# A decoder of state-space scan, cross attention and experts on one core: keys and values made a batch ahead, w2 as seven half-size products, C product in tiles of its own

## The chip, the core and the metric

The kernel runs on one core of a Trainium2 chip. The metric is the device time of one execution in microseconds. The engines of the core run side by side, each with its own instruction queue: TensorE (PE, with its weight loads PEld), VectorE (DVE), ScalarE (ACT), GpSimd (POOL), and SyncE (SP), which here does nothing but issue DMAs. They wait for each other through semaphores. A median is over three runs; the profile is one further execution with every instruction recorded.

## What is computed

Everything is fp32. The input x has 8 batches of 512 tokens of 512 features. Three layers follow one another, each with a sum and a layer norm:

```python
x = layernorm(x + mamba(x))                     # res_scale * (y @ out_proj) + x inside, so 2x + ...
x = layernorm(x + xattn(x, ctx, ctx, mask))
x = layernorm(x + ffn(x))

# mamba: 1024 channels d, 16 states n, token by token
h   = exp(A * dt_t) * h + dt_t * B_t * x_t      # h[d, n]
y_t = sum_n h[d, n] * C_t[n]
# xattn: 16 heads of 32; keys and values come from ctx alone
q, k, v = x @ Wq.T + bq, ctx @ Wk.T + bk, ctx @ Wv.T + bv
# ffn: 32 experts, 4 for each token, at most 640 tokens for an expert
h   = silu(xe @ w1) * (xe @ w3)
out = (h @ w2) * weight                         # added to the token's row
z   = silu(x @ sw1) * (x @ sw3) @ sw2           # the shared expert, for every token
```

## The kernel before

The program has three stages.

**layers** does the scan layer, and beside it attention, the shared expert and the choice of experts. The scan layer runs over 16 chunks, two of 256 tokens for each batch (t = 0 and t = 1). A chunk has 32 steps: for each of 8 groups of 128 channels (c) and each of 4 groups of four states (g). On the 128 partitions lie 64 channels, twice, with two states in each half; so a step's tile h is 128 x (4 x 257), the first column of each row being the state that is carried in. One step is, by engine and line:

- ACT copies the carried state into h's first columns (`carry`, L440; from `state` at t = 1, from zeros at t = 0) and makes the four decays of the next step with Exp (`decays`, L434), into one of two tiles.
- DVE multiplies dt·x with the broadcast B into h (L446), runs the recurrence over h in place (`scan`, L450), at t = 0 copies h's last columns to `state` (L452), and multiplies h by the broadcast C in place (`collect`, L467).
- PE sums the states with eight products of 256 columns into the PSUM tile py (L471).

h has four buffers. The broadcasts of B and C (`bc`, four buffers) come from a scratch in DRAM by SP's DMAs, two steps ahead; the copies of dt and dt·x over the partition halves (`both`) go the same way. Between the steps the loop puts the work around the scan at fixed steps: the gate product (L483), the output projection of the chunk before (L500), the input projections of this chunk's gate and of the next chunk (L302), the convolution (L336), dt (`prepare`).

Attention and the shared expert of batch b − 1 are a list of small pieces, `units(b - 1)`, each with a weight near its PE time. While batch b is scanned, the loop takes pieces from the list as fast as the weights say, so that the list ends with the batch's second chunk. Batch 0 has no such list, and `units(7)` runs after the last chunk, with nothing beside it. A list does, in this order: load Wv and the context (transposed, cT); four products for the values, copied by ACT into `l_va` (L690: per key and pair of heads 32 values, 32 ones, 32 values); four for the keys, to the tile kT with bias and mask (products L682, DVE L702); the first rows of x1, the scan layer's result, from DRAM (`fetch`); their transposes (L676, copy L677); four for the queries; then by pairs of heads `spread` (L722 to L725), which copies queries and keys by DMA into tiles with extra rows for the mask and the maximum, scores and maxima (L735, L737), scores transposed and exponentials (L761, L765), the product with the values (L777); output projection; the shared expert; the choice of experts (`choose`, `locate`); and `send`, which scatters each row to its experts' slots in the buffer xbuf. Large tiles of the list share four slots, s1 to s4: cT and the attention's result are in s2, x1T and then x2's rows in s1, the queries and then the shared expert's hT in s3, kT and then x2T in s4. Every 512 x 512 weight goes through one tile name, wa, with two buffers, loaded one weight ahead.

**experts** goes through the 32 experts. The 640 rows of an expert are loaded at once (xe, L1104) with w1, w3 and w2 (1 MB each, L1107), one expert ahead. `hidden` makes silu(x·w1)·(x·w3) with seven block products instead of eight (Strassen's scheme in Winograd's form) for both weights: 320 columns in each product (L1152), the sums of weight blocks on DVE (`sums_w`, L1127) and of x blocks (`sums_x`, L1144 to L1147), partial sums kept by ACT (L1166) and joined by DVE (L1173, L1177). `give` does the product with w2 in the plain way, five tiles of 128 rows by four products of 512 columns (L1218); ACT scales each tile by the routing weights (L1222) and POOL adds it by an indirect DMA to the tokens' rows in `based` (L1223). Before each of these five tiles PE transposes one tile of the next expert (`flip`, L1136; DVE's copy L1137), and DVE makes one of w3's sums. Each of the five scatters waits for the one before, and an expert's xe tile is read by its scatters until the end, for the row numbers lie in it.

**finish** loads the 4096 rows, and normalizes and stores them (L1266, L1269).

The order of the instructions on each engine is the order in which the program issues them, with a product's use put off by one piece of work (`do`, `settle`); a few places first finish all that is put off (`dry`). The lines of the functions that the change touches follow.

## Time and profile before

| | us |
|---|---|
| median of three runs | 5657.23 (5656.19 to 5658.22) |
| the profiled execution | 5660.41 |
| its span | 5658.7 |

The span is what the profiler saw from the first to the last instruction; mean granted clock of PE 0.937 of full speed.

| stage | from us | to us |
|---|---|---|
| constants, first projections | 0 | 84.9 |
| batch 0, two chunks, nothing beside the scan | 84.9 | 436.4 |
| batch 1 | 436.4 | 901.9 |
| batches 2 to 7, each with attention of the batch before | 901.9 | 3703 |
| attention and shared expert of batch 7 alone | 3703 | 4005 |
| 32 experts, 49.5 us each | 4005 | 5588 |
| finish | 5588 | 5658.7 |

In the steady part a chunk with t = 0 lasts about 226 us, one with t = 1 about 244.

| engine | busy us | share of the span | instructions |
|---|---|---|---|
| PE | 4933.6 | 87% | 18984 |
| PEld | 2576.2 | 46% | 18984 |
| DVE | 4107.3 | 73% | 5290 |
| ACT | 2548.5 | 45% | 5347 |
| POOL | 525.2 | 9% | 424 |

The DMAs moved 744.49 MB in 484,635 packets. The largest groups of instructions, with the busy time of the whole execution and the mean of one:

| line | what | count | busy us | mean ns |
|---|---|---|---|---|
| L450 DVE | scan | 512 | 1172.4 | 2295 |
| L467 DVE | product with C | 512 | 624.1 | 1221 |
| L446 DVE | product with B | 512 | 619.5 | 1217 |
| L434 ACT | decays | 2048 | 894.0 | 499 |
| L471 PE | sum over states | 4096 | 632.4 | 421 |
| L1218 PE | product with w2 | 1280 | 575.1 | 592 |
| L1152 PE | w1 and w3, first form | 1536 | 436.7 | 434 |
| L1222 ACT | scaling of w2's result | 160 | 110.0 | 688 |
| L1223 POOL | scatter | 160 | 252.2 | 1576 |

How to read it: times in a row of the profile are microseconds, and "mean ns" is what one instruction's record lasts; records of products overlap, so that busy time of PE is the union of them. "Idle before, released by" says which other engine's instruction ended the wait.

### The profile page before, as it was taken

What the parts mean: (1) busy time and instruction counts of PE and PEld (TensorE: products, weight loads), DVE (VectorE), ACT (ScalarE), POOL (GpSimd) and SP (SyncE); (2) the same over time, 40 slices, a digit from 0 to 9 for tenths busy, and PEclk for the clock granted to TensorE, in tenths of its full rate; (3) what the DMA queues carried; (4) which work ended last, traced back from release to release, by engine and by line L of the source; (5) the groups of instructions that cost most, each with busy time, mean ns of one, the idle gap of its engine ahead of it and who ended that gap; (6) DMA issues with size and microseconds to landing.
All of it is one profiled execution on the core that took longest, in us unless ns stands there. A gap on an engine that the chain in (4) does not pass through costs nothing. (4 is left out here: it accounts for less than half of the span.)

```text
span 5658.7 us, 57578 instructions
## 1 busy us (share of the span) xinstructions
PE 4933.6 (87%) x18984; PEld 2576.2 (46%) x18984; DVE 4107.3 (73%) x5290; ACT 2548.5 (45%) x5347; POOL 525.2 (9%) x424
## 2 busy tenths in 40 slices
PE   5658889888988988988898898889899999999994
PEld 3334344334434433434443443333566666666662
DVE  5998988989899898898999999834444444444443
ACT  4454565654655456565465646513122222222223
POOL 0000001002000200200200020010211111111111
PEclk8778999999999999999999999999999999999997
DMA  7675345335433634544443363331544444444444
GB/s 205 192 225 176 96 127 164 110 116 158 137 105 108 188 95 127 162 112 117 159 136 105 110 194 94 107 110 43 159 123 115 118 125 115 119 117 123 115 118 137
DMA packets 484635, 744.49 MB, mean 132 GB/s; under 512 B 68170, under 2 KB 200810, under 8 KB 484336
## 3 DMA queue, kind: packets, MB, share of 16 engines
q1 hardware_dynamic: 446832, 655.52, 38.1%
q0 software_dynamic: 33280, 76.90, 7.1%
q10 hardware_dynamic: 4224, 8.39, 0.4%
q8 instruction: 150, 2.46, 0.2%
q14 instruction: 149, 1.22, 0.1%
HBM read 491.91 MB, written 148.28 MB: 113 GB/s over the span
## 5 line engine op out<-in xcount | busy, mean ns | idle before, releaser
L434 ACT ACTIVATE l_da<-both,l_aneg 128x256 f32<-128x256 f32 x2048 | 894.0, 499 | 837.6 <-DVE h L450 795.6
L450 DVE TENSOR_TENSOR_SCAN h<-l_da,h 128x1028 f32<-128x1028 f32 x512 | 1172.4, 2295 | 55.0 <-ACT h L440 28.7
L471 PE MATMUL py<-h,l_twice 128*64 128x256 f32 x4096 | 632.4, 421 | 225.9 <-DVE h L467 225.7
L446 DVE TENSOR_TENSOR h<-both,bc 128x1024 f32<-128x1024 f32 x512 | 619.5, 1217 | 125.2 <-PE py L471 58.3
L467 DVE TENSOR_TENSOR h<-h,bc 128x1024 f32<-128x1024 f32 x512 | 624.1, 1221 | 6.3 <-DVE l_state L452 0.3
L1218 PE MATMUL po<-w,hT 128*128 128x512 f32 x1280 | 575.1, 592 | 0.0
L471 PEld LDWEIGHTS py<-h,l_twice 128*64 128x64 f32 x4096 | 297.9, 147 | 588.1 <-DVE h L467 262.0
L735 PE MATMUL ps_s<-l_ka,l_qa 64*128 64x512 f32 x1024 | 316.9, 698 | 140.8 <-DVE mx L737 140.6
L1152 PE MATMUL ps_h<-xT,w 128*128 128x320 f32 x1536 | 436.7, 434 | 0.0
L1173 DVE TENSOR_TENSOR hT<-ps_h,p 128x320 f32<-128x320 f32 x128 | 63.0, 492 | 443.4 <-PE ps_h L1152 443.4
L1223 POOL DMA_INDIRECT based<-y,xe x160 | 252.2, 1576 | 1358.8 <-ACT y L1222 828.6
L737 DVE TENSOR_REDUCE mx<-ps_s 128x2 f32<-128x1024 f32 x256 | 310.9, 1217 | 81.6 <-PE ps_s L735 81.0
L1222 ACT ACTIVATE y<-po,xe 128x512 f32<-128x512 f32 x160 | 110.0, 688 | 551.7 <-PE po L1218 542.6
L1152 PEld LDWEIGHTS ps_h<-xT,w 128*128 128x128 f32 x1536 | 292.9, 191 | 131.8 <-issue 15.8
L1218 PEld LDWEIGHTS po<-w,hT 128*128 128x128 f32 x1280 | 231.1, 190 | 231.6 <-issue 224.1
L761 PE MATMUL ps_t<-l_qa,l_ka 64*128 64x512 f32 x1024 | 303.3, 655 | 12.9 <-ACT eT L765 9.0
L765 ACT ACTIVATE eT<-ps_t 128x1024 f32<-128x1024 f32 x256 | 258.9, 1013 | 108.3 <-PE ps_t L761 108.0
L777 PE MATMUL po<-eT,l_va 128*64 128x512 f32 x1024 | 278.8, 623 | 21.2 <-ACT raw L789 18.1
L1152 PE MATMUL ps_h<-t,s 128*128 128x320 f32 x1024 | 286.2, 432 | 0.0
L682 PE MATMUL ps_p<-x2T,wa 128*128 128x512 f32 x512 | 249.6, 639 | 21.1 <-DVE hT L852 19.2
L500 PE MATMUL po<-wm,zs 128*128 128x512 f32 x512 | 241.6, 623 | 21.5 <-DMA wm<-in_out_proj_w 21.5
L302 PE MATMUL ps_z<-xnT,wm 128*128 128x256 f32 x1024 | 241.6, 389 | 12.7 <-DMA wm<-in_in_proj_w 12.7
(205 smaller groups left out, 6695.3 us busy)
## 6 DMA issues: line engine op xcount, KB each, us to landing
bc<-scr SPq DMA_DIRECT2D x1024, 128.0 KB
w<-in_w SPq DMA_DIRECT2D x96, 1024.0 KB
wm<-in_in_proj_w SPq DMA_DIRECT2D x128, 512.0 KB
xbuf<-zero SPq DMA_DIRECT2D x32, 1362.5 KB
xe<-xbuf SPq DMA_DIRECT2D x32, 1362.5 KB
both<-dt SPq DMA_DIRECT2D x256, 128.0 KB
both<-dtx SPq DMA_DIRECT2D x256, 128.0 KB
wm<-in_out_proj_w SPq DMA_DIRECT2D x64, 512.0 KB
```

Of the source, the lines that this page charges most:

```text
L434: nc.scalar.activation(da[:, n, 1:], dt[:, c % 2, j, :], AF.Exp, scale=aneg[:, c, j, g, m : m + 1])
L446: nc.vector.tensor_tensor(steps, dtx[:, c % 2].unsqueeze(2).to_broadcast([P, 2, NG // 2, T]), bc[0], ALU.mult)
L450: nc.vector.tensor_tensor_scan(flat, da.rearrange("p n t -> p (n t)"), flat, 0.0, ALU.mult, ALU.add)
L467: nc.vector.tensor_tensor(steps, steps, bc[1], ALU.mult)
L471: nc.tensor.matmul(py[j * HP : (j + 1) * HP, c % 2, :], twice, h[:, j * 2 + m, 1:], start=False, stop=(s == (NST // NG - 1, NG // 2 - 1, 1)),)
L735: nc.tensor.matmul(ps[:, j, :], qa[r, lt * P : (lt + 1) * P], ka[r, :], start=True, stop=True)
L737: return lambda: nc.vector.tensor_reduce(mx[:, lt, :].unsqueeze(2), ps, AX.X, ALU.max) and None
L761: nc.tensor.matmul(ps[:, j, :], ka[r, kc * P : (kc + 1) * P], qa[r, :], start=True, stop=True)
L765: nc.scalar.activation(eT, ps, AF.Exp)
L777: nc.tensor.matmul(po[j * 2 * HD : (j + 1) * 2 * HD, :], va[:, kc, i, j * HD : (j + 2) * HD], eT[:, j, :], start=(kc == 0), stop=(kc == SC ...
L1152: nc.tensor.matmul(ps, w[:, n, r * P : (r + 1) * P], x[:, n, :], start=not more and n == 0, stop=n == 1, skip_group_check=more,)
L1218: nc.tensor.matmul(po, got["hT"][:, ic, j * P : (j + 1) * P], got["w2"][:, ic, :], start=(ic == 0), stop=(ic == DC - 1))
```

## The change

It has four parts.

**w2 by seven products.** Of the five tiles of an expert the first four are done with the same seven-product scheme as w1 and w3, in products of 256 columns: `give` takes hT's first 512 columns as a 2 x 2 block matrix and w2 as another. `sums_w(got, "hT")` makes hT's sums (four DVE instructions of 128 x 512, one in place in hT) at the start of `give`; `sums_w2` makes w2's four during the first half of `hidden`. Results that were scaled by ACT on their way out are now half-width: ACT scales the kept partial sums and two last halves, DVE scales and adds the other six. The fifth tile stays plain. The scatters of the four tiles are issued near the end of `give`, that of the fifth early. The flips of the next expert and w3's sums are taken from the new generator `between` at five places of `give`. hT has one buffer instead of two, y seven instead of six.

**Keys and values a batch ahead.** The new list `sources(b)` holds the loads of Wv, the context, the mask and Wk and the eight products; its results go through the small tile "row" (two buffers) to two DRAM tiles, vd and kd. `units(b)` first takes all but the last two pieces of `sources(b + 1)`, then begins itself with eight DMAs that read vd back into l_va, then takes those two, and reads the keys in `spread` from kd. `sources(0)` is woven into batch 0's own scan, which had no list; `units(7)` has none, and loads Wq in its first piece. kT is gone, and with it the slot s4: x2T goes to s3, hT to s2.

**The product with C and the states.** C's product goes to a new tile hc with three buffers, and h has two buffers instead of four. The copy of the last states moves from DVE to ACT, and from `scan` to `collect`.

**Constants.** `early` and `first` are kept once for four tiles and broadcast; the gate's two comparison tiles lie in one buffer of "row".

```diff
-    early = cp.tile([P, SC, E], F32, name="l_early")
...
+    early = cp.tile([P, E], F32, name="l_early")
+    nc.gpsimd.iota(early, pattern=[[-1, E]], base=E, channel_multiplier=0, allow_small_or_imprecise_dtypes=True)
+    early = early.unsqueeze(1).to_broadcast([P, SC, E])
...
-        h = p3.tile([P, NG, T + 1], F32, tag="h", name="h", bufs=4)
+        h = p3.tile([P, NG, T + 1], F32, tag="h", name="h", bufs=2)
         nc.scalar.copy(h[:, :, 0:1], last if t else nothing)
...
+
+    def collect(t, c, g, h, bc, py, f):
+
         if t < S // T - 1:
-            nc.vector.tensor_copy(state[:, c, g].unsqueeze(2), h[:, :, T : T + 1])
-
-    def collect(c, g, h, bc, py, f):
-
+            nc.scalar.copy(state[:, c, g].unsqueeze(2), h[:, :, T : T + 1])
 
...
         steps = h.rearrange("p (j m) t -> p j m t", j=2)[:, :, :, 1:]
-        nc.vector.tensor_tensor(steps, steps, bc[1], ALU.mult)
+        hc = p3.tile([P, NG, T], F32, tag="hc", name="hc", bufs=3)
+        nc.vector.tensor_tensor(hc.rearrange("p (j m) t -> p j m t", j=2), steps, bc[1], ALU.mult)
...
                     twice,
-                    h[:, j * 2 + m, 1:],
+                    hc[:, j * 2 + m, :],
...
+    kept = {}
+
+    def sources(b):
+
+        st, todo = {}, []
+
+        def begin():
             load("Wv")
             st["cT"] = cT = quad("s2", "cT")
             nc.sync.dma_start(cT, rows(a["ctx"][b]))
             st["mk"] = mk = p1.tile([P, S], U8, tag="mk", name="mk")
             nc.sync.dma_start(mk, a["mask"][b : b + 1, :].to_broadcast([P, S]))
+            kept[b] = [dp.tile([S, D], F32, tag="vd", name="vd"), dp.tile([D, S], F32, tag="kd", name="kd")]
+
+        def values(pc):
+            if pc == 0:
+                load("Wk")
+            w, cT = loaded["Wv"], st["cT"]
+            ps = dense(lambda dc: cT[:, dc, pc * P : (pc + 1) * P], lambda dc: w[:, dc, :])
+
+            def put():
+                v = p3.tile([P, D], F32, tag="row", name="v")
+                nc.scalar.copy(v, ps)
+                nc.sync.dma_start(kept[b][0][pc * P : (pc + 1) * P, :], v)
+
+            return put
+
+        def keys(oc):
+            if oc == 0 and b:
+                load("Wq")
+            w, cT = loaded["Wk"], st["cT"]
+            ps = dense(lambda dc: w[:, dc, oc * P : (oc + 1) * P], lambda dc: cT[:, dc, :])
+
+            def put():
+
+                k = p3.tile([P, D], F32, tag="row", name="k")
+                nc.vector.scalar_tensor_tensor(k, ps, bk[:, oc : oc + 1], st["mk"], ALU.add, ALU.mult)
+                nc.sync.dma_start(kept[b][1][oc * P : (oc + 1) * P, :], k)
+
+            return put
+
+        todo.append((0, begin, False))
+        for j in range(SC):
+            todo.append((3.4, lambda j=j: values(j), False))
+        for j in range(DC):
+            todo.append((3.4, lambda j=j: keys(j), False))
+        return todo
+
+    def dense(lhs, rhs):
+        ps = psm.tile([P, S], F32, tag="mm", name="ps_p")
+        for dc in range(DC):
+            nc.tensor.matmul(ps, lhs(dc), rhs(dc), start=(dc == 0), stop=(dc == DC - 1))
+        return ps
+
+    def units(b):
+
+        st = {}
...
+        def begin():
+            if b == B - 1:
+                load("Wq")
             st["x1T"] = quad("s1", "x1T")
+            vd, st["kd"] = kept.pop(b)
+            for pc in range(SC):
+                for j in range(2):
+                    nc.sync.dma_start(
+                        va[:, pc, :, 2 * j * HD : (2 * j + 1) * HD],
+                        vd[pc * P : (pc + 1) * P, :].rearrange("p (i j d) -> p i j d", j=2, d=HD)[:, :, j, :],
+                    )
...
                 nc.sync.dma_start(qa[r1 : r1 + HD, :], st["qT"][r0 : r0 + HD, i // 2, :])
-                nc.sync.dma_start(ka[r1 : r1 + HD, :], st["kT"][r0 : r0 + HD, i // 2, :])
+                h0 = (2 * i + j) * HD
+                nc.sync.dma_start(ka[r1 : r1 + HD, :], st["kd"][h0 : h0 + HD, :])
...
-                st["x2T"] = quad("s4", "x2T")
...
-                st["hT"] = quad("s3", "hT")
...
-        for j in range(SC):
-            add(3.4, values, j)
-        for j in range(DC):
-            add(3.4, keys, j)
-            if j == 2:
-                add(0, fetch, 0)
+        more = sources(b + 1) if b + 1 < B else []
+        todo += more[:-2]
+        add(0, begin)
+        add(0, fetch, 0)
+        todo += more[-2:]
...
-        if t == 0 and b:
-            side, spent = units(b - 1), 0.0
+        if t == 0:
+            side, spent = units(b - 1) if b else sources(0), 0.0
...
+    def BW(w, j, k):
+        return w[:, 2 * j : 2 * j + 2, k * FH : (k + 1) * FH]
...
-        s1, s2, s4 = (wp.tile([P, 2, FH], F32, tag=f"{n}s{i}", name="s") for i in (1, 2, 4))
+        s1, s2, s4 = (wp.tile([P, 2, FH], F32, tag=f"{n}s{i}", name="s", bufs=1 if n == "hT" else 2) for i in (1, 2, 4))
...
+
+    def sums_w2(got):
+
+        w = got["w2"]
+        got["t2"] = t1, t2, t3, t4 = [wp.tile([P, 2, FH], F32, tag=f"w2t{i}", name="t", bufs=1) for i in range(4)]
+        for o, x, y in (
+            (t1, BW(w, 0, 1), BW(w, 0, 0)),
+            (t2, BW(w, 1, 1), t1),
+            (t3, BW(w, 1, 1), BW(w, 0, 1)),
+            (t4, BW(w, 1, 0), t2),
+        ):
+            nc.vector.tensor_tensor(o, x, y, ALU.subtract)
+            yield
...
-    def give(e, got, j):
-
-        xe = got["x"]
+    def give(e, got, side):
+
+        xe, hT, w2 = got["x"], got["hT"], got["w2"]
+        t1, t2, t3, t4 = got["t2"]
+        both = range(2)
+        ys = [p2.tile([P, D], F32, tag="y", name="y", bufs=CJ + 2) for j in range(CJ)]
...
+        def keep(ps, r, tag, j):
+            v = p2.tile([P, HALF], F32, tag=f"{tag}{r}", name=tag)[:, 0:FH]
+            nc.scalar.activation(v, ps, AF.Identity, scale=weight(j))
+            return v
+
+        def use(j, k, ps, more):
+            nc.vector.scalar_tensor_tensor(ys[j][:, k * FH : (k + 1) * FH], ps, weight(j), more, ALU.mult, ALU.add)
...
+        def put(j):
...
+            )
+
+        for _ in sums_w(got, "hT"):
+            pass
+        s1, s2, s3, s4 = got["hT", "s"]
+        next(side, None)
+        xs, p1, pu, p5 = [], [], [], []
+        for r in both:
+            xs.append(psx.tile([P, HALF], F32, tag="h", name="ps_o")[:, 0:FH])
+            product(xs[r], A(hT, 0, 0), r, BW(w2, 0, 0))
+            p1.append(keep(xs[r], r, "p1", r))
+
+        j = CJ - 1
         po = pso.tile([P, D], F32, tag="po", name="po")
         for ic in range(DC):
-            nc.tensor.matmul(
-                po, got["hT"][:, ic, j * P : (j + 1) * P], got["w2"][:, ic, :], start=(ic == 0), stop=(ic == DC - 1)
-            )
-        y = p2.tile([P, D], F32, tag="y", name="y", bufs=CJ + 1)
-        nc.scalar.activation(y, po, AF.Identity, scale=xe[:, j, D + e : D + e + 1])
-        nc.gpsimd.indirect_dma_start(
-            out=based,
-            out_offset=bass.IndirectOffsetOnAxis(ap=xe.bitcast(I32)[:, j, D + E :], axis=0),
-            in_=y,
-            in_offset=None,
-            bounds_check=N + P - 1,
-            compute_op=ALU.add,
-        )
+            nc.tensor.matmul(po, hT[:, ic, j * P : (j + 1) * P], w2[:, ic, :], start=(ic == 0), stop=(ic == DC - 1))
+        nc.scalar.activation(ys[j], po, AF.Identity, scale=weight(j))
+        put(j)
+        next(side, None)
+        for r in both:
+            ps = psy.tile([P, HALF], F32, tag="h2", name="ps_o")[:, 0:FH]
+            product(ps, A(hT, 0, 1), r, BW(w2, 1, 0))
+            use(r, 0, ps, p1[r])
+        for r in both:
+            product(xs[r], s2, r, t2, more=True)
+            pu.append(keep(xs[r], r, "pu", r))
+        next(side, None)
+        zs = []
+        for r in both:
+            zs.append(psy.tile([P, HALF], F32, tag="h2", name="ps_o")[:, 0:FH])
+            product(zs[r], s1, r, t1)
+            p5.append(keep(zs[r], r, "p5", 2 + r))
+        for r in both:
+            product(xs[r], s3, r, t3, more=True)
+            use(2 + r, 1, xs[r], p5[r])
+        next(side, None)
+        for r in both:
+            product(zs[r], s4, r, BW(w2, 1, 1), more=True)
+            use(r, 1, zs[r], pu[r])
+            put(r)
+        next(side, None)
+        for r in both:
+            product(xs[r], A(hT, 1, 1), r, t4, more=True)
+            nc.scalar.activation(ys[2 + r][:, 0:FH], xs[r], AF.Identity, scale=weight(2 + r))
+            put(2 + r)
+
+    def between(nxt):
+
+        sums = sums_w(nxt, "w3")
+        for j in range(CJ):
+            flip(nxt, j)
+            if j == CJ - 1:
+                sums_x(nxt)
+            next(sums, None)
+            yield
 
     nxt = load(0)
     for j in range(CJ):
@@ -1238,20 +1347,10 @@
             pass
     for e in range(E):
         got, nxt = nxt, load(e + 1) if e + 1 < E else None
-        got["hT"] = p2.tile([P, DC, CAP], F32, tag="hT", name="hT")
+        got["hT"] = p2.tile([P, DC, CAP], F32, tag="hT", name="hT", bufs=1)
         for r in range(2):
-            hidden(got, r, sums_w(nxt, "w1") if nxt and r else iter(()))
-        side = sums_w(nxt, "w3") if nxt else iter(())
-
-        for n, j in enumerate(reversed(range(CJ))):
-            if nxt:
-                flip(nxt, n)
-                if n == CJ - 1:
-                    sums_x(nxt)
-            next(side, None)
-            give(e, got, j)
-        for _ in side:
-            pass
+            hidden(got, r, sums_w2(got) if r == 0 else sums_w(nxt, "w1") if nxt else iter(()))
+        give(e, got, between(nxt) if nxt else iter(()))
```

In the changed kernel's numbering the product with B is L447, the scan L451, the copy of the states L456, the product with C L469, the sum over states L473; the store of the values L674, the keys L687 with their store L688, the reload of the values L717, the keys' reading L753; in the experts the sums are L1160 and L1192, the block products L1198, the plain tile L1300.

## The prediction

> **What bounds the kernel now.** I read the stages first, from busy times in stretches that I cut at the first scan of a chunk and at the last product.
>
> ```profile
> core 0: us, PE busy (x) PEld busy (x) DVE busy (x) ACT busy (x) POOL busy (x), PEclk, DMA share, GB/s
> 84.90:436.40 351.50, 211.13 (x916) 115.20 (x916) 337.43 (x335) 190.31 (x452) 17.14 (x12) 0.74 0.69 207
> ...
> 657.00:3703.00 3046.00, 2658.83 (x10884) 1256.51 (x10882) 2751.07 (x3198) 1710.90 (x3622) 207.91 (x173) 0.94 0.44 129
> 3703.00:4005.00 302.00, 255.84 (x805) 103.86 (x806) 101.64 (x194) 67.88 (x90) 32.00 (x35) 0.90 0.30 98
> 4005.00:5588.00 1583.00, 1582.69 (x5484) 984.79 (x5483) 665.15 (x1175) 392.48 (x801) 249.13 (x158) 1.00 0.45 115
> ```
>
> Batch 0's scans (first row) are DVE: 96% of it. The steady layers (second) are DVE 90% and PE 87%, each waiting for the other by turns. The last batch's attention alone (third) is PE with gaps. The experts (fourth) are PE and nothing else: no idle in 1583 us, at full clock.
>
> Then one expert, in order of time:
>
> ```profile
> 4711.17 0.37 SPq L1104 DMA_DIRECT2D xe<-xbuf  x1
> ...
> 4728.71 0.60 PE L1136 MATMUL ps_t<-e_ident,xe 128*128 128x128 f32 x4
> ...
> 4729.15 3.60 PE L1218 MATMUL po<-w,hT 128*128 128x512 f32 x8
> ...
> 4733.01 0.69 DVE L1127 TENSOR_TENSOR s<-w 128x512 f32<-128x512 f32 x1 [2.95 <-DMA w<-in_w]
> 4733.02 3.60 PE L1218 MATMUL po<-w,hT 128*128 128x512 f32 x8
> ...
> 4739.19 1.54 POOL L1223 DMA_INDIRECT based<-y,xe  x1 [3.91 <-DMA based<-y,xe]
> ...
> 4744.43 1.54 POOL L1223 DMA_INDIRECT based<-y,xe  x1 [3.69 <-DMA based<-y,xe]
> ```
>
> An fp32 product is two matmul records; four flips and eight records repeat every 3.87 us. The scatters run one behind the other, 5.4 us apart, and the next rows (xe) are fetched when the last has landed.
>
> **w2 as seven products.** The records of 512 columns take (3.87 − 0.43 for the flips)/8 = 0.43 us. What a record of 256 columns costs at full clock shows in the layers:
>
> ```profile
> 999.93 3.62 PE L302 MATMUL ps_x<-xnT,wm 128*128 128x256 f32 x16
> ```
>
> (3.62 − 0.38 for the last one's own length)/15 = 0.216 us, half of 0.43, so narrow products lose nothing and the weight loads (190 ns) still fit under them. Before: 5 × 8 × 0.43 = 17.2 us an expert. After: one tile plainly, 8 × 0.43 = 3.44, and 7 products × 2 row blocks × 2 × 2 records = 56 × 0.216 = 12.1; 15.54. Gain 1.66 us, over 31 experts 51.5.
>
> This needs DVE and DMA in time. DVE gets 8 sums of 0.69 us (L1127's duration) and 6 half-width evictions of 0.48 (L336, 256 wide): 8.4 us more on 665/32 = 20.8, of a 47.8 us expert. In the order that the changed kernel queues, counted from the first flip (t = 0): last multiply of hT 1.0, flip copy 1.75, hT's four sums until 4.3, four sums of the weights two experts ahead, which DVE in the second fence waited for until 4.6, so until 7.0; flip copy 7.7, one sum 8.3, first eviction of the second PSUM pair 8.75. PE wants that PSUM at 10.2: 1.4 us to spare. The last hT sum is wanted at 14, t2 of the next x a good 3 us after it is made. The scatters bunch: one at 6.6, then two at 16 and two at 18, so the last issues at 33 and lands at 38; give ends at 18, hence xe is fetched 20 us into the next hidden stage where it was 12.6, takes 5.7 us, and is wanted at 29.5: 3.8 us spare. SP's next loads (w1 two experts on) wait for that stage's end anyway. ACT's 4.1 us for 3.4 has room (25% busy). In the last expert the bunch is exposed: last fetch 35 us after give's start (14.0 + 3 × 5.3 + 5.1), before 30.8: +4.2. Net **−47.3**, bounds 0 (PE loses what it gains) and −51.5.
>
> [...]
>
> **Keys and values a batch ahead.** In the steady layers eight products of a next batch replace eight of this one: no PE change. The last batch alone loses them:
>
> ```profile
> 3745.44 13.90 PE L682 MATMUL ps_p<-wa,cT 128*128 128x512 f32 x32
> ...
> 3759.18 13.90 PE L682 MATMUL ps_p<-cT,wa 128*128 128x512 f32 x32
> ...
> 3779.39 1.94 PE L676 MATMUL ps_tr<-l_ident,xr 128*128 128x128 f32 x8 [4.82 <-DMA xr<-x1d]
> ...
> 3782.01 15.76 PE L682 MATMUL ps_p<-x1T,wa 128*128 128x512 f32 x32 [0.68 <-ACT x1T L677]
> ```
>
> 27.5 us go, but they covered the norm, store and reload of the last x1 rows. ACT's norm ends 3750.56; I give store plus reload 7 us (the 1 MB load above took 5.2, here 0.75 MB in two steps), two flips and a copy 2.5: queries at 3760, **−22**, bounds −10 (a round trip of 19) and −33 (none). Batch 0 now holds them: PE is 60% busy there, so they hide; if that cover is gone they cost 27.5. DVE's four evictions (0.75) count: **+3**.
>
> Moved DMAs: per batch 8 stores, 8 reloads of va, with ka read from DRAM instead of SBUF in the same number. SP spends about 0.6 us on an issue (bc pairs 1.1 to 1.2 in the trace), so 16 × 0.6 = 9.6 us of SP a batch. The reloads are 8192 pieces of 128 B; in the trace's DMA records 4608 packets of that size took 12 ns each: 6.2 us a batch over 16 engines. Queued behind are bc loads, whose buffers come free three scans (some 20 us) before they are used, and behind those DVE. I take 10 us over the run, bounds 0 and 77 (all SP time, 8 batches): **+10**. cT now waits until the shared product has freed its tile, as Wk did before; PE has a projection of 16 products and gate products queued first: 0, or 5.2 × 7 = 36 uncovered, inside that bound.
>
> [...]
>
> **State and C product.**
>
> ```profile
> L440 ACT COPY h<-l_state 128x4 f32<-128x4 f32 x256 | 47.4, 190 | 140.1 <-PE py L471 140.0
> ...
> L452 DVE COPY l_state<-h 128x4 f32<-128x4 f32 x256 | 42.0, 165 | 2.4
> ```
>
> Those are two groups of instructions: busy time, mean ns of one, idle time before them. The next are waits of DVE in the steady layers: total, times, longest.
>
> ```profile
> DVE h L446 <- PE py L471: 57.1, 24, 7.8
> ...
> DVE h L450 <- ACT h L440: 26.7, 16, 2.9
> ...
> DVE h L450 <- ACT l_da L434: 11.2, 13, 2.4
> ```
>
> A copy and its gap take 0.205 us of DVE between scan and product (2.54 from one to the next with it, 2.33 without): 256 × 0.205 = 52.5. DVE is 90% busy but half its phases end on PE; I count 60%: **−31**, bounds 0 and −52.5. On ACT they cost 256 × 0.19 = 49 us, behind waits that the next decays have anyway (the same scan): 0, at worst another 11. Behind the waiting copy stand the next h's first column and decays. With h freed by DVE, ACT no longer waits for PE at L440: up to −27. In its place DVE's C product waits for the third last PE group; the lead is about 2.9 us shorter (the product itself and side work), worst another 57. Those two I set against each other: **0**. The gate's shared tile and broadcast constants keep their instructions: 0.
>
> **Sum.** −47.3 − 22 + 3 + 10 − 31 = −87. The profiled execution took 5660.41 (span 5658.7 and 1.7 around it): 5573. It stood 3.2 above the median of the runs shown, so the forecast is 5570.
>
> **The rivals.** (1) *The experts give nothing* (13%). DVE stands behind weights that land late. Each us past 1.4 stalls PE in every expert; at 3.1 us later the gain is gone: 5570 + 47 = 5617. For: DVE waits there already. Against: landing has 0.3 us to come, not 3. (2) *The batch's start turns slower* (16%). SP holds 16 more issues and stores that wait for PE's evictions, bc lands late, DVE stops. From 12.5 us a batch (87/7) it decides; at 20 us a batch, 5570 + 140 − 10 = 5700, slower. For: SP's queue is served in order and DVE already waits for bc and dtx (38 us). Against: 20 us of lead. (3) *Buffers take back DVE's gain* (12%): shorter lead on PE in every phase change, +31 and half of 57: 5630; with only the first, 5601.
>
> **How the numbers follow.** My forecast holds 59%, its own range 5530 to 5605. Faster by over 0.2% (11 us, about what this kernel's measurement tells from none): the forecast, rival 1 and rival 3 without the worst of its bound (4 of its 12%, near no change): 0.80; slower 0.16, rival 2; between 0.04. The range reaches down to 5515 (−33 and −52.5 whole, ACT's wait gone) and up to 5660, which leaves out rival 2's body.
>
> **What would show it.** Experts 47.8 us apart with PE without idle; no DVE record of the state copy, 256 more on ACT; the last queries some 22 us sooner after the last projection; bc waits near 17 us in total. A PE idle before the second pair of half-width products, DVE waits on bc of 10 us a batch, or DVE's C product waiting for PE over 100 us, would prove me wrong.

## The result and the profile after

The changed kernel took 5680.34 us (median of five, 5678.28 to 5691.67) against 5658.22 (five, 5656.19 to 5668.76): ratio 1.0038, interval 1.0024 to 1.0053. It is slower by 22 us, where 87 less were forecast. The stages of the two profiled executions, cut at the starts of the first and the last scan, of the first weight load of the experts and of the last expert, and at the end:

| stage | before us | after us | difference | forecast |
|---|---|---|---|---|
| layers, first to last scan | 3616.7 | 3699.2 | +82.5 | −18 |
| last batch's attention | 300.8 | 284.1 | −16.7 | −22 |
| 31 experts | 1537.4 | 1486.7 | −50.7 | −51.5 |
| last expert and finish | 118.9 | 123.0 | +4.1 | +4.2 |

The experts went as forecast to within 1 us and the last batch to within 6; nearly the whole miss is in the layers. The busy times in stretches, cut as before (columns as there):

```profile
core 0: us, PE busy (x) PEld busy (x) DVE busy (x) ACT busy (x) POOL busy (x), PEclk, DMA share, GB/s
83.80:445.90 362.10, 241.01 (x980) 126.53 (x980) 338.61 (x308) 196.80 (x488) 21.82 (x12) 0.76 0.71 213
679.90:3783.00 3103.10, 2678.55 (x10876) 1264.96 (x10873) 2720.58 (x2997) 1744.86 (x3817) 223.13 (x173) 0.93 0.45 133
3783.00:4070.00 287.00, 229.08 (x750) 92.07 (x751) 104.74 (x204) 65.74 (x87) 31.99 (x35) 0.88 0.30 102
4070.00:5600.00 1530.00, 1529.39 (x6252) 1129.70 (x6250) 901.27 (x1619) 426.00 (x929) 246.49 (x157) 1.00 0.47 118
```

In the second row, the steady layers, DVE does less than before (2720.58 for 2751.07) and yet the stretch is longer (3103 for 3046): DVE's idle time grew from 295 to 383 us. In the fourth PE is idle for 0.6 us of 1530, with DVE at 59%. The experts by time:

```profile
4809.62 0.37 SPq L1134 DMA_DIRECT2D xe<-xbuf  x1
...
4820.54 3.60 PE L1300 MATMUL po<-w,hT 128*128 128x512 f32 x8
...
4830.03 1.89 PE L1198 MATMUL ps_o<-t,hT 128*128 128x256 f32 x8
4830.23 0.69 DVE L1192 TENSOR_TENSOR t<-w 128x512 f32<-128x512 f32 x1 [0.56 <-PE ps_o L1198]
```

Eight records of 256 columns take 1.89 us, eight of 512 take 3.60: about half, as forecast. The next rows (xe) are fetched 21.6 us into the hidden stage, whose first weight load is at 4788.0, where the prediction had 20. The last batch's products (start, duration, idle before and its releaser), with the last projection before, whose queries the prediction shows at 3782.01:

```profile
3735.81 9.80 PE L500 MATMUL po<-wm,zs 128*128 128x512 f32 x16 [4.92 <-DMA wm<-in_out_proj_w]
```

and after:

```profile
3820.98 8.83 PE L502 MATMUL po<-wm,zs 128*128 128x512 f32 x16 [7.44 <-DMA wm<-in_out_proj_w]
...
3840.47 1.94 PE L732 MATMUL ps_tr<-l_ident,xr 128*128 128x128 f32 x8 [9.16 <-DMA xr<-x1d]
3843.09 16.59 PE L702 MATMUL ps_p<-x1T,wa 128*128 128x512 f32 x32 [0.67 <-ACT x1T L733]
```

The queries begin 13.3 us after the last projection, before 36.4: the round trip over x1 that values and keys had covered now stands bare (9.16 us), and 23 are won. Some are lost again: PE waits 7.44 us for the projection's weights, 4.92 before, so that the queries come 20.3 us sooner when counted from the last scan.

Where the layers lost it, no single row says. The group of the state copies (whole run), then ACT's waits and some of DVE's in the steady layers (waits: total, times, longest):

```profile
L456 ACT COPY l_state<-h 128x4 f32<-128x4 f32 x256 | 50.1, 196 | 477.2 <-DVE h L451 477.1
```

```profile
ACT l_state L456 <- DVE h L451: 383.4, 150, 7.8
ACT l_da L435 <- DVE h L451: 247.6, 126, 5.2
ACT h L441 <- DVE hc L469: 241.8, 168, 12.1
...
ACT h L441 <- DVE mv L74: 74.5, 7, 13.4
```

Rows of before that the prediction does not show, for ACT's copy of the carried state and for DVE's dt·x and first tap of the convolution:

```profile
ACT h L440 <- PE py L471: 158.9, 92, 5.3
...
DVE h L446 <- DMA both<-dtx: 29.4, 14, 3.5
...
DVE xs L336 <- ACT xs L328: 18.5, 14, 2.4
```

DVE after:

```profile
DVE h L447 <- DMA both<-dtx: 58.4, 20, 6.7
DVE xs L337 <- ACT xs L329: 37.3, 18, 3.6
DVE hc L469 <- PE py L473: 37.2, 31, 2.6
DVE h L451 <- ACT l_da L435: 35.9, 13, 5.2
```

DVE waits for PE less than before (37.2 at C for 57.1 at B). It waits longer for what comes late by way of ACT and the DMAs: dt·x (58.4 for 29.4), the convolution's first tap (37.3 for 18.5), the decays (35.9 for 11.2). And DVE's order has changed. Before, a step's C product mostly stood ahead of the next scan, as here in the first chunk of batch 5:

```profile
2450.71 2.30 DVE L450 TENSOR_TENSOR_SCAN h<-l_da,h 128x1028 f32<-128x1028 f32 x1
...
2455.24 1.22 DVE L446 TENSOR_TENSOR h<-both,bc 128x1024 f32<-128x1024 f32 x1
2456.37 1.22 DVE L467 TENSOR_TENSOR h<-h,bc 128x1024 f32<-128x1024 f32 x1
2457.51 2.29 DVE L450 TENSOR_TENSOR_SCAN h<-l_da,h 128x1028 f32<-128x1028 f32 x1
```

After, in the first chunk of the same batch:

```profile
2425.00 2.36 DVE L447 TENSOR_TENSOR h<-both,bc 128x1024 f32<-128x1024 f32 x2 [0.78 <-DMA both<-dtx]
2427.28 4.48 DVE L451 TENSOR_TENSOR_SCAN h<-l_da,h 128x1028 f32<-128x1028 f32 x2
2431.68 2.33 DVE L469 TENSOR_TENSOR hc<-h,bc 128x1024 f32<-128x1024 f32 x2
2433.93 2.35 DVE L447 TENSOR_TENSOR h<-both,bc 128x1024 f32<-128x1024 f32 x2
2436.20 4.48 DVE L451 TENSOR_TENSOR_SCAN h<-l_da,h 128x1028 f32<-128x1028 f32 x2
```

Two B products, two scans, two C products. Pairs occur before as well, at this very step too (two scans from 2428.11), so the count decides. Over the 352 steps of batches 2 to 7 without the very last chunk, a scan starts ahead of the C product of the step before in 36 of them before (10%) and in 167 after (47%). So what was said above, that the engines' order is the program's, is not so. The order on an engine is chosen when the kernel is built, by the framework's scheduler, and the number of buffers enters that choice: among the runs below, h3 and hc4 change nothing but one such number, and their scans run ahead in 61% and 29% of the same steps.

### The profile page after: what moved, and what is told of

Same layout as the page of the kernel before. It is cut to its first block, busy times and chain, and to the rows that moved or that the text cites. A ratio compares the mean times of both kernels' runs of the same rounds, so it can differ in the third digit from the quotient of the medians.

```text
span 5676.8 us, 60761 instructions
## 1 busy us (share of the span) xinstructions
PE 4912.7 (87%) x19752; PEld 2731.2 (48%) x19752; DVE 4314.2 (76%) x5482; ACT 2625.7 (46%) x5737; POOL 540.6 (10%) x424
## 5 line engine op out<-in xcount | busy, mean ns | idle before, releaser
L451 DVE TENSOR_TENSOR_SCAN h<-l_da,h 128x1028 f32<-128x1028 f32 x512 | 1170.2, 2294 | 59.0 <-ACT l_da L435 35.9
L473 PE MATMUL py<-hc,l_twice 128*64 128x256 f32 x4096 | 636.4, 427 | 205.0 <-DVE hc L469 204.9
L447 DVE TENSOR_TENSOR h<-both,bc 128x1024 f32<-128x1024 f32 x512 | 617.7, 1220 | 111.3 <-DMA both<-dtx 58.4
L469 DVE TENSOR_TENSOR hc<-h,bc 128x1024 f32<-128x1024 f32 x512 | 620.7, 1217 | 45.4 <-PE py L473 41.8
L473 PEld LDWEIGHTS py<-hc,l_twice 128*64 128x64 f32 x4096 | 301.5, 150 | 574.5 <-DVE hc L469 252.0
L765 PE MATMUL ps_s<-l_ka,l_qa 64*128 64x512 f32 x1024 | 334.6, 709 | 117.2 <-DVE mx L767 116.4
L1198 PE MATMUL ps_h<-xT,w 128*128 128x320 f32 x1536 | 435.9, 433 | 0.0
L1198 PEld LDWEIGHTS ps_h<-xT,w 128*128 128x128 f32 x1536 | 292.5, 191 | 118.5 <-issue 0.8
L1198 PE MATMUL ps_h<-t,s 128*128 128x320 f32 x1024 | 286.1, 432 | 0.0
L502 PE MATMUL po<-wm,zs 128*128 128x512 f32 x512 | 249.2, 642 | 37.2 <-DMA wm<-in_out_proj_w 35.9
L456 ACT COPY l_state<-h 128x4 f32<-128x4 f32 x256 | 50.1, 196 | 477.2 <-DVE h L451 477.1
L640 POOL DMA_INDIRECT xbuf<-x2t,dest x128 | 198.7, 1553 | 693.4 <-DVE dest L634 599.3
L303 PE MATMUL ps_x<-xnT,wm 128*128 128x256 f32 x1024 | 245.7, 394 | 2.0 <-ACT xnT L292 1.6
```

What stands on the lines that cost most here:

```text
L303: nc.tensor.matmul(ps[:, i, :], w[:, dc, i * P : (i + 1) * P], f["xnT"][:, dc, :], start=(dc == 0), stop=(dc == DC - 1),)
L447: nc.vector.tensor_tensor(steps, dtx[:, c % 2].unsqueeze(2).to_broadcast([P, 2, NG // 2, T]), bc[0], ALU.mult)
L451: nc.vector.tensor_tensor_scan(flat, da.rearrange("p n t -> p (n t)"), flat, 0.0, ALU.mult, ALU.add)
L469: nc.vector.tensor_tensor(hc.rearrange("p (j m) t -> p j m t", j=2), steps, bc[1], ALU.mult)
L473: nc.tensor.matmul(py[j * HP : (j + 1) * HP, c % 2, :], twice, hc[:, j * 2 + m, :], start=False, stop=(s == (NST // NG - 1, NG // 2 - 1, 1)),)
L765: nc.tensor.matmul(ps[:, j, :], qa[r, lt * P : (lt + 1) * P], ka[r, :], start=True, stop=True)
```

## The experiments

Each ratio is to the kernel before, timed beside it, with its interval; "layers" is first to last scan of the one profiled execution. The letters in the expectations are rival accounts of the layers' loss. A: the third part of the change (tile, buffers, copy). B: keys and values ahead. C: the state copy on ScalarE. D: two h buffers make ScalarE wait for DVE's C product. E: DVE's C product has too short a lead over PE. F: the order of issue. G: ScalarE stands before its copy of the carried state, which waits for DVE's C product. H: a tile or a buffer costs by itself.

**The parts apart.** w2_alone: the experts of the changed kernel, all else before.

> Edit: the kernel before with only the experts of the changed kernel (w2 as seven products); layers as before. All theories agree on the layers (first to last scan 3617 us as before, 3699 in the changed kernel). Theory: the seven products give what the changed kernel's trace shows, 1.63 us an expert over 31, less 4 in the last: 5658 - 46 = 5612. Rival: the experts' gain hangs on the layers' change (memory, state of the queues): then not below 5640.

5614.85 us, 0.9923 (0.9901 to 0.9946); 47.96 us an expert, layers 3606. The gain stands on its own. The layers are the same code as before, which took 3616.7 there: one profiled execution can differ by some 10 us.

no_c: the changed kernel with

```diff
-        h = p3.tile([P, NG, T + 1], F32, tag="h", name="h", bufs=2)
+        h = p3.tile([P, NG, T + 1], F32, tag="h", name="h", bufs=4)
...
-        hc = p3.tile([P, NG, T], F32, tag="hc", name="hc", bufs=3)
-        nc.vector.tensor_tensor(hc.rearrange("p (j m) t -> p j m t", j=2), steps, bc[1], ALU.mult)
+        nc.vector.tensor_tensor(steps, steps, bc[1], ALU.mult)
...
-            nc.scalar.copy(state[:, c, g].unsqueeze(2), h[:, :, T : T + 1])
+            nc.vector.tensor_copy(state[:, c, g].unsqueeze(2), h[:, :, T : T + 1])
```

> Edit: the changed kernel with the product with C in place in h again (four buffers) and the states copied by DVE; keys and values a batch ahead and w2 stay. Theory A (two h buffers, the extra tile and the copy on ScalarE cost the layers' 82 us): layers 3630 us, near 3617 plus the 13 that the prediction gave to the keys' DMAs; time 5658 - 46 - 17 + 13 = 5608. Theory B (the keys and values a batch ahead cost them): layers stay at 3690 or more, time 5670 or more. Half and half: layers 3660, time 5640.

5618.34 us, 0.9925 (0.9909 to 0.9942); layers 3638, attention 281.4. So the keys ahead cost 21 us in the layers and won 19 in the last batch, each to some 10 us; in the medians they won nothing (5618.34 with them, 5614.85 without). The third part cost 61 in the layers and 62 in the medians.

hc_copydve keeps hc and two h buffers, with only the copy back on DVE in `scan`; inplace_copyact keeps the copy on ScalarE, with C in place and four h buffers.

> Edit: the changed kernel with only the copy of the last states back on DVE, right behind the scan. Theory C (the copy holds up ScalarE's queue and with it evictions, the gate's Silu and dt): t = 0 chunks return to 227 us from 233, layers some 3650, time 5630. Theory A with the buffers as cause, or theory B: layers stay near 3699 or get longer by up to half of the 52 us that the copies take on DVE, time 5680 to 5705.

5685.91 us, 1.0045 (1.0032 to 1.0059); layers 3699.

> Edit: the changed kernel with the product with C in place in h, four buffers, but the states still copied by ScalarE, so that DVE's product with C has to wait for that copy. Theory A with the buffers as cause: layers near 3630 to 3650, time 5610 to 5630. Theory B: 5670 or more. Theory C: 5680 or more, for DVE now waits for ScalarE in each step as well.

5618.13 us, 0.9925 (0.9909 to 0.9942); layers 3639. Which engine copies the states makes no difference either way; theory C falls. (With the copy on DVE, PE's order in batches 3 to 6 is that of the changed kernel, instruction by instruction.) The loss comes with the tile and the buffers; the two were not tried apart, with C in place and two h buffers.

**Buffers.** h3: `name="h", bufs=3`. hc4: `name="hc", bufs=4`. inplace_h3: no_c with `bufs=3` for h. pinned:

```diff
-        nc.vector.tensor_tensor(
+        tc.keep_in_program_order(nc.vector.tensor_tensor(
             steps, dtx[:, c % 2].unsqueeze(2).to_broadcast([P, 2, NG // 2, T]), bc[0], ALU.mult
-        )
+        ))
```

> Edit: the changed kernel with three h buffers instead of two. With the keys ahead and w2, but C in place, the layers (first to last scan) took 3638 us; the changed kernel 3699. Theory D (two h buffers: ScalarE's copy into the next h, and with it its queue, waits for DVE's product with C): h is now free one step earlier; at least 40 of the 61 us come back, layers 3660 or less, time 5640 or less. Theory E (DVE's product with C waits for PE three groups back, a lead too short): nothing comes back, 5675 to 5685. Theory F (the order in which the scheduler issues B product, scan and C product, in pairs): the build has 133 places with two B products in a row against 113 in the changed kernel, so nothing comes back or it gets worse.

5736.84 us, 1.0139 (1.0121 to 1.0157): 56 slower than with two.

> Edit: the changed kernel with four hc buffers instead of three. Theory E: the 37 us for which DVE waits at the product with C go and with them most of the 61 us, time 5620 to 5645. Theory D: nothing comes back, 5675 to 5685. Theory F: 129 pairs against 113, nothing comes back.

5765.9 us, 1.0195 (1.0178 to 1.0212): 85 slower than with three. More buffers make it worse, so that neither D nor E, a wait for want of a buffer, explains the 61 us. But the share of scans that run ahead does not rank the kernels either: hc4 has 29% to the changed kernel's 47%, and is slower.

> Edit: the changed kernel with each product with B pinned behind what the program put before it on DVE, which is the product with C of the step before, so that B, scan and C alternate (no pairs in the build). Theory F: most of the 61 us come back, time 5620 to 5645. Theories D and E: not better than 5670; since DVE then may not use a wait for other work, up to 5720.

5645.03 us, 0.9981 (0.9972 to 0.9991), the slow end of F's range; 35 of the 61 are back. No scan runs ahead here.

> Edit: the changed kernel with C in place in h and the states copied by DVE, but three h buffers instead of four (with four: 5618). Theory E (a lead of three groups over PE is too short): slower by most of 61 us, 5660 to 5685. Theory D (ScalarE waits for DVE): with three buffers and C in place h comes free when PE is done, so ScalarE waits longer too, 5630 to 5660. Theory F: 93 pairs as in the kernel before (95): 5618 to 5630.

5659.48 us, 1.001 (1.0001 to 1.002): 41 slower than with four. Theory F, which forecast 5618 to 5630, missed; 5659 lies on the border between D's range and E's. A scan runs ahead in only 5% of the steps here. So where C is in place a buffer less does cost, and the scans that run ahead are not what costs; whether a wait or the rest of the order does is not shown.

**Is it ScalarE's place before the carry?** pool_carry and no_c_pool_carry: `nc.gpsimd.tensor_copy` for `nc.scalar.copy` in `carry`, in the changed kernel and in no_c. hc4_pinned and no_c_pinned: the pin of B on hc4 and on no_c.

> Edit: four hc buffers and each product with B pinned behind the product with C of the step before. Unpinned, the fourth hc buffer cost 85 us (5766); with three and the pin the kernel took 5645. Theory F (buffers act only through the order in which the scheduler then issues DVE's work): 5630 to 5650, the fourth buffer gives DVE a little more lead. Theory E, or buffers that cost by themselves: 5700 or more.

5791.67 us, 1.0234 (1.0217 to 1.0251). A miss for F, and the number lies where E, or buffers that cost by themselves, had it. No scan runs ahead. The pin holds B behind C, but in batches 3 to 6 the orders on DVE, ScalarE and PE still differ from those of the pinned kernel with three buffers, so that order and buffer are not told apart here; lin_c_hc4 below tries that.

> Edit: the changed kernel with C in place in h, four buffers, states copied by DVE (unpinned 5618), and the same pin of B behind C. Theory F: with the same order on DVE the separate tile costs nothing and saves DVE's copies, so this one is no faster than the kernel with hc and the pin: 5640 to 5675. Theory G (ScalarE stands before its copy into the next h, which waits for DVE's product with C): in place h comes free with PE, four groups back, so it stays at 5618 to 5635, faster than hc with the pin (5645).

5693.1 us, 1.0051 (1.0032 to 1.007). Under this pin the separate tile is 48 us faster than in place, unpinned 62 slower: the sign hangs on the order. It came out slower than F's range, and far from the 5618 to 5635 of theory G. With C in place the pin alone cost 75 us, so that what pinned won back is net of what a pin costs.

> Edit: the changed kernel with the copy of the carried states into the next h on GpSimd instead of ScalarE; the build has 120 places with two B products in a row against 113. Theory G: PE's and DVE's waits for ScalarE (93 and 101 us in four batches) fall to what they are with C in place (31 and 58), layers 3640 to 3655, time 5620 to 5640. Theory F: the order is the changed kernel's or slightly worse, 5675 to 5700.

5759.2 us, 1.0173 (1.0156 to 1.019).

> Edit: C in place, four buffers, states copied by DVE (5618), and the copy of the carried states on GpSimd. Theory G: ScalarE hardly stood there for long (4 us at most), so 5610 to 5622. Theory F: the order is nearly the same (108 pairs against 104), 5612 to 5630.

5695.34 us, 1.0063 (1.0044 to 1.0082). Both are slower than either theory had them, and neither tells what it was made for. In four batches of pool_carry DVE waits:

```profile
DVE h L451 <- issue: 63.6, 4, 17.7
```

Once in each batch the small copy stands on GpSimd behind the 16 scatters of `send`, and the scan behind it for up to 17.7 us: the row names no releaser ("issue"), but at 965 us the copy starts as the sixteenth scatter ends, at 964.8, and the scan follows at 965.0. In no_c_pool_carry one such wait, of 13.9 us, is put down to GpSimd's copy itself. The two kernels lost 79 and 77 us, so no gain shows beside that for the one that theory G meant. G isn't shown false, but nothing speaks for it.

**One order for all.** lin_c, lin_no_c and lin_c_hc4 add at the end of `layers`:

```diff
+    last = {}
+    for i in nc.cur_bb.bb.instructions:
+        if type(i).__name__ in ("BassTilePoolBoundary", "InstRegisterMove"):
+            continue
+        if i.engine in last and str(i.engine).split(".")[-1] in ('PE', 'DVE', 'Activation'):
+            tc.add_manual_dep(
+                i, last[i.engine].name,
+                mybir.DependencyInfo(mybir.DependencyClass.NoSync, mybir.DependencyReason.DATA),
+                reason="program order",
+            )
+        last[i.engine] = i
```

> Edit: the changed kernel with the instructions of PE, DVE and ScalarE held in the order of the program in all of the layers. Theory F (the buffers act through the order in which the scheduler issues the engines' work; in one fixed order the separate tile only saves DVE its copies): faster than the same order with C in place (lin_no_c), by 10 to 50 us. Rival H (a separate product tile, fewer h buffers or the copy on ScalarE cost time by themselves): slower than lin_no_c by about 60 us, as without the fixed order (5682 against 5618). How fast either is depends on how good the program's order is: 5600 to 5750.

6727.71 us, 1.1895 (1.1868 to 1.1922).

> Edit: C in place, four h buffers, states copied by DVE, keys ahead and w2 as in the changed kernel, the three engines held in the order of the program in the layers. Theory F: slower than lin_c by 10 to 50 us. Rival H: faster than lin_c by about 60 us.

6719.98 us, 1.188 (1.1855 to 1.1905).

> Edit: lin_c with four hc buffers. The order of PE, DVE and ScalarE is the same, instruction by instruction, so only the buffer differs. Theory F: as lin_c or up to 20 us faster, where the scheduler's own order made the fourth buffer cost 85 us (5766 against 5681), and 147 with B alone pinned. Rival H (a buffer costs by itself): 60 us or more slower than lin_c.

6732.32 us, 1.1897 (1.187 to 1.1924). In batches 3 to 6 the order on all three engines is the same in lin_c and lin_c_hc4. In one order the tile with the copy costs 8 us and a fourth buffer 5, within the intervals, so rival H with its 60 falls; the 10 to 50 us that F gave the tile don't show either. A caution: in this order the engines wait for each other far longer (layers 4752 to 4769 us), so that some difference may be hidden in its waits.

**The deferred product alone.** scan_behind: the changed kernel with one restraint; `newest` is a list to which `collect` appends C's product.

```diff
-        nc.vector.tensor_tensor_scan(flat, da.rearrange("p n t -> p (n t)"), flat, 0.0, ALU.mult, ALU.add)
+        sc = nc.vector.tensor_tensor_scan(flat, da.rearrange("p n t -> p (n t)"), flat, 0.0, ALU.mult, ALU.add)
+        if newest:
+            tc.add_manual_dep(
+                sc.ins, newest[-1].ins.name,
+                mybir.DependencyInfo(mybir.DependencyClass.NoSync, mybir.DependencyReason.DATA),
+                reason="program order",
+            )
```

> Edit: the changed kernel with one restraint: each scan is queued on DVE behind the product with C of the step before (47% of the scans in four of its batches' traces start before it, 10% with C in place). Narrow form of theory F (the deferred product with C alone is the loss, since PE's sums and the release of the broadcasts wait for it): most of the 61 us come back, 5620 to 5645. Wide form (the whole order differs, this only being its most visible part): less than half comes back, 5650 to 5700.

5582.18 us, 0.9863 (0.9841 to 0.9886): 98 us faster than the changed kernel, the fastest of all, and faster than both forms of F forecast: the narrow one had no more than the 61 us come back. DVE's order in it:

```profile
2386.03 2.36 DVE L447 TENSOR_TENSOR h<-both,bc 128x1024 f32<-128x1024 f32 x2 [1.16 <-DMA both<-dtx]
2388.31 2.29 DVE L451 TENSOR_TENSOR_SCAN h<-l_da,h 128x1028 f32<-128x1028 f32 x1
2390.70 1.23 DVE L477 TENSOR_TENSOR hc<-h,bc 128x1024 f32<-128x1024 f32 x1
2391.84 2.29 DVE L451 TENSOR_TENSOR_SCAN h<-l_da,h 128x1028 f32<-128x1028 f32 x1
```

B may still run ahead, the scan no more. The restraint moves other work too: in batches 3 to 6 the orders on PE and ScalarE differ from the changed kernel's as well. no_c_behind and hc4_behind put the same restraint on C in place and on four hc buffers.

> Edit: C in place, four h buffers, states copied by DVE (5618), with the same restraint. If the restraint undoes what the separate tile brought about, it does little here, where 10% of the scans start ahead of the product with C: 5605 to 5625, and the separate tile with the restraint (5582) is then worth 25 to 40 us, near the 31 that the prediction gave to the copies. If the restraint is a gain of its own, 5560 to 5590.

5620.84 us, 0.9932 (0.9918 to 0.9946), as no_c, with the same order on PE in batches 3 to 6. The restraint is no gain of its own: it undoes what the tile brought about.

> Edit: the restraint of scan_behind (a scan is queued on DVE behind the product with C of the step before; 5582) and four hc buffers. If the deferred product with C is the loss that the fourth buffer made worse (5766 without the restraint, against 5681 with three), it is now 5575 to 5610. If the fourth buffer costs through the rest of the order, 5640 or more.

5701.57 us, 1.0077 (1.0064 to 1.0089). 64 us better than hc4, and still 119 slower than three buffers: this is the case that was forecast for a fourth buffer that costs through the rest of the order, and the deferred C is only a part of its loss.

What the restraint changed, batches 3 to 6, one profiled execution each (that of scan_behind is the slowest of its four, 5598.14 us); waits are sums over the trace's rows:

| kernel | us | DVE busy | DVE waits for ACT / DMA / PE | PE waits for DVE / ACT |
|---|---|---|---|---|
| before | 1881 | 1702 | 40 / 34 / 83 | 178 / 25 |
| no_c | 1889 | 1706 | 58 / 43 / 58 | 172 / 31 |
| after | 1925 | 1686 | 101 / 60 / 61 | 138 / 93 |
| scan_behind | 1877 | 1673 | 73 / 31 / 91 | 136 / 59 |

In the changed kernel DVE waits 161 us for ACT and the DMAs and 61 for PE; in scan_behind it waits 104 and 91, and PE waits less for ACT (59 for 93). The end of a dt stage in the second chunk of batch 4 is one example. After:

```profile
2284.41 2.29 DVE L451 TENSOR_TENSOR_SCAN h<-l_da,h 128x1028 f32<-128x1028 f32 x1
...
2295.03 0.69 DVE L413 TENSOR_TENSOR dtx<-dt,xs 128x512 f32<-128x512 f32 x1
...
2301.71 2.36 DVE L447 TENSOR_TENSOR h<-both,bc 128x1024 f32<-128x1024 f32 x2 [3.73 <-DMA both<-dtx]
2305.29 2.30 DVE L451 TENSOR_TENSOR_SCAN h<-l_da,h 128x1028 f32<-128x1028 f32 x1 [1.22 <-ACT l_da L435]
```

and scan_behind at the same steps:

```profile
2259.46 0.68 DVE L413 TENSOR_TENSOR dtx<-dt,xs 128x512 f32<-128x512 f32 x1
...
2260.13 2.29 DVE L451 TENSOR_TENSOR_SCAN h<-l_da,h 128x1028 f32<-128x1028 f32 x1
...
2268.69 0.69 DVE L493 TENSOR_TENSOR zs<-zs,py 128x512 f32<-128x512 f32 x1 [4.34 <-PE py L481]
2269.29 2.35 DVE L447 TENSOR_TENSOR h<-both,bc 128x1024 f32<-128x1024 f32 x2
2271.56 2.29 DVE L451 TENSOR_TENSOR_SCAN h<-l_da,h 128x1028 f32<-128x1028 f32 x1
```

dt·x (L413) has to go through a DMA and the decays before the next channels can be scanned. After, the last scan that could have filled that time began 10.6 us before dt·x, ahead of the side work; DVE stands 3.73 and 1.22 us. In scan_behind a scan lies in the gap. DVE stands there too, 4.34 us, but for PE's sums, at the gate product (L493), and the next scan starts without a wait. From dt·x to that scan 10.3 us pass after and 12.1 in scan_behind, where a scan and a C product (3.5 us) are done in the meantime: an estimate from these rows is that 1.7 us are won. The scan at 2284.41 does not itself run ahead of a C product; the example shows what the other order does at one place, and not how the 98 us add up.

## Why the prediction was wrong

- *w2 as seven products*: right. −47.3 forecast, −46.6 measured (−50.7 and +4.1), with 256 columns at half of 512, DVE in time and xe within 2 us of its forecast place. Rival 1 (the experts give nothing) did not come.
- *The last batch*: −22 forecast, −16.7 here and −19.4 in no_c. The mechanism was right, the bare round trip too (queries 23 us sooner).
- *Keys ahead*: +13 forecast, +21 measured, 8 of it in batch 0, where the forecast had 3. Mis-sized. In no_c, where the keys ahead stand without the third part, batches 0 and 1 hold 17 of the 21, and DVE's wait for bc over the whole run is as before (17.9 us, 17.6 before; 27.1 in the changed kernel, "near 17" was forecast). The reloads' pieces of 128 B took 13.2 ns each, 6.7 us a batch for the 6.2 forecast. So the 10 us put down for SP's issues don't show at bc, and what batch 1 lost is not known. Rival 2 came nearest in time (5700) but not in mechanism.
- *State copy*: −31 forecast on DVE, and nothing on ACT. Moved alone, with C in place or not, it gave 0 (5618.13 for 5618.34, 5685.91 for 5680). DVE's 165 ns went and the time did not, so the 60% of the copies' time that the forecast counted as on the path was too much; by how much each place waits for DVE was not measured. With the scan held behind C in both, tile and copy together gave 39 us (5620.84 to 5582.18), near the forecast.
- **The step that failed** is "Those two I set against each other: **0**". It weighed two waits on PE, and these were small indeed (37.2 us at C, forecast at up to 57). Over the wait on PE it missed that the new tile and buffer counts change the order in which the work is queued: C deferred behind the next scan in 47% of the steps. In place of 0 the tile and the buffers cost 62 us (5618.34 to 5680.34), with the copy's move worth nothing. ACT's wait at the carry didn't go either; it turned from PE (158.9 us) to DVE (241.8 and 74.5, up to 13.4 at once), though DVE's own wait behind it fell from 26.7 to 10.7. Rival 3 had the place but priced it by waits: 5601 to 5630, where the layers alone lost 61.
- Its own test, "DVE's C product waiting for PE over 100 us", did not fire though the forecast was wrong (37.2 us), nor did its two others. They watched for waits and not for the order.

Shown is that C in its own tile loses through the order, since one restraint on the order, with the same tiles and buffers, turns +62 into −39. That the deferred C product is the part of the order that costs is the likeliest reading, but not shown alone: the restraint moves work on PE and ScalarE too, pinned has no deferred C either and won back only 35, and hc4 has fewer than the changed kernel and is slower. Left open is the fourth buffer's 119 us under the restraint. One trait goes with most of the loss: in batches 1 to 6 the last products of the shared expert stand later in PE's order than in no_c, counted in steps of the sum over states, by 2.1 after, 2.7 in h3, hc4 and hc4_behind, 3.6 in hc4_pinned, but by 0.6 in scan_behind and 0.7 in pinned. Against it stands no_c_pinned, with 1.1 and a loss of 75 us. That it is the cause was not tried. Nor was theory G, beyond GpSimd.

## What to carry to other kernels

Where a scheduler orders the queues, a buffer count is an edit of the order: compare the issue order of the built kernels (how often does work run ahead of what feeds another engine?) before pricing waits. Here DVE had less to do and the layers took longer, until one edge kept it from running ahead of the product that PE waits for; the same edge did nothing where few scans ran ahead, and holding B behind C cost 75 us. Take a change of several parts apart early: of these, one gained 46 us, one gave nothing and one lost 61 that a restraint turned into 39 won.

## What the runs showed of the hardware

PE's busy time for the same 6736 to 6737 matmul records in batches 3 to 6 was 1653.5 us in no_c and 1676.97 in hc4, at granted clocks of 0.94 and 0.92 (0.87 over the whole of lin_c). So the clock can be a part of hc4's loss: an estimate is at most the 23.5 us by which PE was busy longer, of 87. Less clock did not always go with more time: pinned took 1907 us for these batches at 0.929, the changed kernel 1925 at 0.935. ScalarE's records of the 128x4 copy of the carried state last 195 ns in the changed kernel; in pool_carry, with the copy on GpSimd behind its scatters, DVE's scan waited up to 17.7 us at once.
